# Graph network, four layers: the last chunk's adjacency in blocks of 32 rows, the reciprocals' transpose later, the first projection by quarters

## The chip, the cores and the metric

The kernel runs on one core of one Trainium2 chip. The metric is the device time of one execution in microseconds; smaller is better. Before and after are compared by the median of several executions.

## The reference

Four layers act on N = 2708 nodes with D = 512 features and a dense 2708 x 2708 adjacency matrix of zeros and ones, all in float32. The edits lie in layer 0, an attention layer with 8 heads of 64 dimensions:

```python
mask = adj, with ones on the diagonal
for h in range(8):
    q, k, v = x @ Wq[h], x @ Wk[h], x @ Wv[h]          # 2708 x 64 each
    s = where(mask > 0, q @ k.T / sqrt(64), -1e16)      # 2708 x 2708
    heads[h] = softmax(s, axis=-1) @ v                  # 2708 x 64
x = layernorm(x + sum(heads[h] @ Wo[h] for h in range(8)))
```

This is the computation in short form, with the mask as the kernel applies it. Layers 1 to 3 are a sum over neighbours with two linear maps, a second attention over the edges and a graph convolution scaled by node degree (the row sums of adj). They use the degrees that layer 0 collects on the way.

## The kernel before

**Tiling.** The nodes fall into NC = 22 chunks of 128 rows. The last chunk, LAST = 21, has only LR = 20 rows. The heads are taken as four pairs p; a pair's two heads are j = 0 and 1, in the lower and the upper 64 partitions. Over the columns of the score matrix there are three batches k: 1024, 1024 and 660 columns.

**The projections.** Before the attention, six blocks b of up to 512 nodes are projected to KT (psk), V (psv) and the queries (psq), which go to DRAM as qtd. `load_rows` brings a weight matrix or a block xb of the transposed features in one DMA of 1 MB. `project_in` multiplies, for one of four output groups p, the four feature quarters k into one PSUM tile; the pool ps_0 has four such tiles. `evac` copies to SBUF on DVE and ACT in turn.

**The attention loop.** It runs over items (c, p): 84 items for the 21 full chunks and one for the last chunk, in which four groups of 32 partitions hold the four pairs of heads of the 20 rows. Twelve of the 32 rows are filling: rows of chunk 20 that are computed and not used. An iteration works on several items at once: `scores` of the new item (PE products at line 310 and a fused add-and-maximum on DVE at L332), `weights` of the one before (exponentials on ACT, L354), `blocks` (transposes of 32 x 32 blocks on DVE, L361, into a tile d), `deal` (eight DMAs that reorder d into e, L371), `values` (products with V on PE, L417), and `turn` (PE transposes of the third batch, copied by ACT at L391 to L401). The results ot go to DRAM (otd), for the last chunk as otz (L481, L482).

**The next chunk's adjacency.** While the four items of chunk c run, `load_chunk(c + 1, p)` fetches one batch of adjacency columns per item (L167, for the last chunk L172) and, in the fourth item, the queries qt (L176, L178). `row_sums` adds up the batch on ACT into dgp (L185), from which the degrees come, `loops` puts ones on the diagonal (L197), and `mask` turns zeros into -1e16. For the last chunk, each of the four groups of 32 partitions gets the 20 real rows at its partitions 0 to 19, and 12 rows of chunk 20 behind them: two DMAs for each group and each batch.

**Sums and reciprocals.** The exponentials' sums are collected in smt. `heads_sums` adds them and forms reciprocals for the chunks 0 to 10 and later for 11 to 20 (L490, L495). `heads_rows` turns these by a PE transpose (prs, L503), copies them on ACT (rst, L505) and stores them to rs_d (L506). `last_sums` does so for the last chunk (L511 to L517: rz, prz, rstz, rz_d). The epilogue from L664 on loads otd, x and the reciprocals broadcast over 64 partitions (rb, L673), multiplies on POOL (L674), projects by wo on PE (L677) and normalises.

**Order.** Within the attention loop the order of PE, DVE and ACT is the order of the code. SP issues nearly all DMAs and POOL a few; on these two a scheduler orders the work by its own estimate of when it is ready. The degree computation (L595 to L600) is written after the loop; the scheduler places it on DVE and ACT within the last iterations. A queue works in order: a DMA whose issue waits holds what stands behind it. The main loop's lines:

```python
for i in range(len(items) + 3):
    ...
    if i in (HALF0 * NP + 2, len(items)):
        sums = heads_sums(i == len(items))
    if cur is not None:
        cur.turn()
    if i in (HALF0 * NP + 3, len(items)):
        heads_rows(*sums)
    if i == len(items) + 1:
        last_sums()
    old, late, cur = late, cur, new
```

Of the kernel before, what the change touches and what calls it, by code (L numbers as in the profile page):

```python
# [8 lines left out]
F32 = mybir.dt.float32  # L9
AF = mybir.ActivationFunctionType  # L10
# [5 lines left out]
P = 128  # L16
BLK = 512
# [5 lines left out]
def kernel(  # L23
# [22 lines left out]
    nc = tc.nc  # L46
    N, D = x.shape
    KD = 64
    NP = wq.shape[1] // P
    KC = D // P  # L50
# [4 lines left out]
    def rows(c):  # L55
        return c * P, min(P, N - c * P)
# [8 lines left out]
    const = ctx.enter_context(tc.tile_pool(name="const", bufs=1))  # L65
# [46 lines left out]
    def load_rows(t, src):  # L112
        nc.sync.dma_start(t, src.rearrange("(k p) f -> p k f", p=P))


    NW = 3
# [5 lines left out]
    nc.vector.memset(far, -1e16)  # L122
    dgp = const.tile([P, NC, NW], F32, tag="dgp", name="dgp")
    nc.vector.memset(dgp, 0.0)
    HALF0 = NC // 2
    smt = [const.tile([P, HALF0, 2 * NP, NW], F32, tag=f"smt{i}", name=f"smt{i}") for i in range(2)]
    for t in smt:
# [4 lines left out]
    rz_d = dram.tile([2, NP, 32], F32, tag="rz_d", name="rz_d")  # L132
    LAST = NC - 1
    LR = N - LAST * P
    otd = [dram.tile([P, NP, rows(c)[1]], F32, tag=f"otd{c}", name=f"otd{c}") for c in range(NC)]
    with ExitStack() as l0:
        kvp = l0.enter_context(tc.tile_pool(name="kv", bufs=1))
# [8 lines left out]
        qtd = [dram.tile([P, NP, rows(c)[1]], F32, tag=f"qtd{c}", name=f"qtd{c}") for c in range(NC)]  # L146
# [9 lines left out]
        def load_chunk(c, k):  # L156

            r0, q = rows(c)
            if k == 0:
                a = adjp.tile([P, N], F32, tag="adj", name=f"adj{c}")  # L160
                qt = io.tile([P, NP, P], F32, tag="qt", name=f"qt{c}")
                loaded[c] = (a, qt)
            a, qt = loaded[c]
            if k < NW:
                n0, w = batch(k)
                if c < LAST:
                    nc.sync.dma_start(a[:q, n0 : n0 + w], adj[r0 : r0 + q, n0 : n0 + w])  # L167
                    return

                for g in range(NP):  # L170
                    for d, r, n in ((0, r0, LR), (LR, N - 32, 32 - LR)):
                        nc.sync.dma_start(  # L172
                            a[32 * g + d : 32 * g + d + n, n0 : n0 + w], adj[r : r + n, n0 : n0 + w]
                        )
            else:
                nc.sync.dma_start(qt[:, :, :q], qtd[c])  # L176
                if c == LAST:
                    nc.sync.dma_start(qt[:, :, q:32], qtd[c - 1][:, :, P - (32 - q) :])  # L178

        def row_sums(c, k):  # L180

            r0, q = rows(c)
            a = loaded[c][0]
            n0, w = batch(k)
            nc.scalar.activation(  # L185
                a[:q, n0 : n0 + w], a[:q, n0 : n0 + w], AF.Copy, accum_out=dgp[:q, c, k : k + 1]
            )

        def loops(c, k):

            r0, q = rows(c)
            a = loaded[c][0]
            n0, w = batch(k)
            if n0 <= r0 < n0 + w:
                for g in range(0, P, 32) if c == LAST else (0,):
                    d = a[g : g + q, r0 : r0 + q]
                    nc.vector.tensor_tensor(d, d, ident[g : g + q, g : g + q], ALU.max)  # L197
# [7 lines left out]
        with tc.tile_pool(name="kvw", bufs=1) as kvw, tc.tile_pool(name="xTb", bufs=2) as xtp, tc.tile_pool(  # L205
            name="ps_0", bufs=4, space=PSUM
        ) as ps_0:
            wk_sb = kvw.tile([P, KC, D], F32, tag="wk", name="wk_sb")
            wv_sb = kvw.tile([P, KC, D], F32, tag="wv", name="wv_sb")
            wq_sb = kvw.tile([P, KC, D], F32, tag="wq", name="wq_sb")  # L210
            load_rows(wk_sb, wk)
            for b in range(NB):
                n0, w = cols(b)
                xb = xtp.tile([P, KC, BLK], F32, tag="xb", name=f"xb{b}")
                load_rows(xb[:, :, :w], xT[:, n0 : n0 + w])
                if b == 0:
                    load_rows(wv_sb, wv)
                    load_rows(wq_sb, wq)

                def project_in(w_sb, p, name):  # L220
                    ps = ps_0.tile([P, BLK], F32, tag="t", name=name)
                    for k in range(KC):
                        nc.tensor.matmul(  # L223
                            ps[:, :w],
                            w_sb[:, k, p * P : (p + 1) * P],
                            xb[:, k, :w],
                            start=(k == 0),
                            stop=(k == KC - 1),
                        )
                    return ps  # L230

                for p in range(NP):
                    ps = project_in(wk_sb, p, f"psk{b}_{p}")
                    evac(KT[:, p, n0 : n0 + w], ps[:, :w])


                xp = xtp.tile([P, KC, BLK], F32, tag="xp", name=f"xp{b}", bufs=1)
                for c in chunks_of(b):
                    o, q = rows(c)[0] - n0, rows(c)[1]
                    src = xb[:, :, o : o + q]  # L240
                    dst = xp[:, :, o : o + q]
                    if c < ND:
                        src = src.rearrange("p k (i x) -> p k x i", i=KD4)
                        dst = dst.rearrange("p k (x i) -> p k x i", i=KD4)
                    nc.gpsimd.tensor_copy(dst, src)
                for c in chunks_of(b):
                    r0, q = rows(c)
                    ps = ps_0.tile([P, BLK], F32, tag="t", name=f"psv{c}")
                    for k in range(KC):
                        nc.tensor.matmul(  # L250
                            ps[:q, :],
                            xp[:, k, r0 - n0 : r0 - n0 + q],
                            wv_sb[:, k, :],
                            start=(k == 0),
                            stop=(k == KC - 1),
                        )
                    evac(V[:q, c, :], ps[:q, :])
                qb = xtp.tile([P, NP, BLK], F32, tag="qb", name=f"qb{b}")
                for p in range(NP):
                    ps = project_in(wq_sb, p, f"psq{b}_{p}")  # L260
                    nc.scalar.mul(qb[:, p, :w], ps[:, :w], QSCALE)
                for c in chunks_of(b):
                    r0, q = rows(c)
                    nc.gpsimd.dma_start(qtd[c], qb[:, :, r0 - n0 : r0 - n0 + q])
                if b == NB - 3:
                    for k in range(NW + 1):
                        load_chunk(0, k)
                    for k in range(NW):
                        row_sums(0, k)
                        loops(0, k)  # L270
                        mask(0, k)

            ga_sb = kvw.tile([P, D], F32, tag="ga", name="ga_sb")
            pr = kvw.tile([P, D], F32, tag="pr", name="pr")
            nc.sync.dma_start(ga_sb, ga.partition_broadcast(P))
            for k in range(2 * KC):
                gw_sb = kvw.tile([P, D], F32, tag="gw", name=f"gw{k}", bufs=2)
                nc.sync.dma_start(gw_sb, gw[k * P : (k + 1) * P, :])
                nc.vector.tensor_tensor(pr, gw_sb, ga_sb, ALU.mult)
                nc.vector.tensor_reduce(u[:, k : k + 1], pr, AX.X, ALU.add)  # L280
# [159 lines left out]
        class Last(Pair):  # L440
# [18 lines left out]

            def weight(self, m, p, j):  # L460
                if m >= ND:
                    return self.pts[m, j][:, 32 * p : 32 * p + LR]
                f = max(f for f in self.E if f <= m)
                return self.E[f][:, p, j, m - f, :LR]

            def values(self, m0, m1):
                if self.done == 0:
# [52 lines left out]
        items = [(c, p) for c in range(LAST) for p in range(NP)] + [(LAST, 0)]  # L520
        old = late = cur = None
        with tc.manual_schedule(
            engines={mybir.EngineType.PE, mybir.EngineType.DVE, mybir.EngineType.Activation}
        ):
            for i in range(len(items) + 3):
# [4 lines left out]
                if i < len(items):  # L530
                    c, p = items[i]
# [35 lines left out]
                    sums = heads_sums(i == len(items))  # L567
                if cur is not None:
                    cur.turn()
                if i in (HALF0 * NP + 3, len(items)):  # L570
                    heads_rows(*sums)
                if i == len(items) + 1:
                    last_sums()
# [84 lines left out]
    with tc.tile_pool(name="wo", bufs=1, reuse_waits="tile") as wop:  # L658
        wo_sb = wop.tile([P, KC, D], F32, tag="wo", name="wo_sb")
        load_rows(wo_sb, wo)  # L660
        for c in range(NC):
            r0, q = rows(c)
# [4 lines left out]
            heads = rz_d if c == LAST else rs_d[c >= HALF0][c % HALF0]  # L667
            heads = heads.rearrange("j p q -> j (p q)")
            for j in range(2):
                dst = rb[j * KD : (j + 1) * KD]  # L670
                dst = dst[:, :, :32] if c == LAST else dst.rearrange("k p q -> k (p q)")
                src = rz_d[j] if c == LAST else heads[j]
                nc.sync.dma_start(dst, src.partition_broadcast(KD))  # L673
            nc.gpsimd.tensor_tensor(ot[:, :, :q], ot[:, :, :q], rb[:, :, :q], ALU.mult)  # L674
            po = ps_acc.tile([P, BLK], F32, tag="acc", name=f"po{c}")
# [122 lines left out]
    if True:  # L798
# [19 lines left out]
        for c in range(NC):  # L818
            q = rows(c)[1]
# [489 lines left out]
```

## Time and profile before

| what | us |
|---|---|
| median of 3 executions | 2607.38 |
| lowest and highest of the 3 | 2600.11 and 2610.36 |
| the profiled execution | 2611.59 |
| its span in the profile | 2609.8 |
| PE busy in the span | 2540.3 |
| DVE busy | 1874.5 |
| ACT busy | 1212.1 |
| POOL busy | 312.0 |

All times of the profile belong to that one execution and count from the start of its span. A row names the engine, the line of the kernel, the operation, its output and inputs, the shapes and how often (x). "[1.90 <-DVE rz L511]" means that the engine stood idle for 1.90 us before, and that the work named ended the idle time. The engines are PE (matrix products; PEld its weight loads), DVE, ACT, POOL and SP, which issues DMAs ("SPq" in the chain and in the rows of issues). "issue" as a releaser means that the profile shows nothing that was waited for. Ends of PE's records are modelled, so a busy PE is not always one at its peak.

### The profile page before, as it was taken

What the parts mean: (1) busy time and instruction counts of PE and PEld (TensorE: products, weight loads), DVE (VectorE), ACT (ScalarE), POOL (GpSimd) and SP (SyncE); (2) the same over time, 40 slices, a digit from 0 to 9 for tenths busy, and PEclk for the clock granted to TensorE, in tenths of its full rate; (3) what the DMA queues carried; (4) which work ended last, traced back from release to release, by engine and by line L of the source; (5) the groups of instructions that cost most, each with busy time, mean ns of one, the idle gap of its engine ahead of it and who ended that gap; (6) DMA issues with size and microseconds to landing.
All of it is one profiled execution on the core that took longest, in us unless ns stands there. A gap on an engine that the chain in (4) does not pass through costs nothing.

```text
span 2609.8 us, 42027 instructions
## 1 busy us (share of the span) xinstructions
PE 2540.3 (97%) x15263; PEld 1472.2 (56%) x15263; DVE 1874.5 (72%) x4576; ACT 1212.1 (46%) x2417; POOL 312.0 (12%) x322
## 2 busy tenths in 40 slices
PE   8999999999999999999899999899999999999997
PEld 3445666767676766676546444444444456444465
DVE  2004999999999999998484678978767775453544
ACT  1113778788787787887211001566555640000000
POOL 1110000000000000000220000234333330000000
PEclk9999999999999999999899999989999999999999
DMA  5012888888988888888772544354434213644633
GB/s 199 32 53 58 215 230 217 222 220 209 240 206 210 229 217 216 229 209 184 208 219 76 134 119 139 112 166 135 123 100 129 62 30 108 180 143 141 181 100 107
DMA packets 221445, 411.45 MB, mean 158 GB/s; under 512 B 28711, under 2 KB 48857, under 8 KB 221238
## 3 DMA queue, kind: packets, MB, share of 16 engines
q1 hardware_dynamic: 214998, 392.03, 56.3%
q0 software_dynamic: 6240, 16.73, 1.8%
q8 instruction: 121, 1.98, 0.3%
q14 instruction: 86, 0.70, 0.1%
HBM read 213.57 MB, written 16.72 MB: 88 GB/s over the span
## 4 chain that ended last, share of the span: by engine, by line
PE 77%; issue 9%; DVE 6%; DMA 4%; SPq 2%; ACT 1%; POOL 0%; POOLq 0%; DVEq 0%; ACTq 0%
PE pss L310 15%; PE av L417 14%; PE acc L731 13%; PE acc L837 7%; PE m L1141 6%; PE pf L743 3%; PE psv L250 3%; PE psk L223 3%; PE pst L390 3%; PE psq L223 3%; DMA e<-d 2%; PE po L677 2%; PE ph L823 1%; DVE d L361 1%; SPq L371 1%
## 5 line engine op out<-in xcount | busy, mean ns | idle before, releaser
L332 DVE CUSTOM_DVE_ANT_0 s<-pss,adj 128x512 f32<-128x512 f32 (+1 forms) x1020 | 574.2, 618 | 27.6 <-PE pss L310 26.5
L354 ACT ACTIVATE s<-s,nm 128x1024 f32<-128x1024 f32 (+1 forms) x510 | 527.7, 1037 | 22.9 <-DVE nm L347 22.0
L310 PE MATMUL pss<-KT,qt 64*128 64x512 f32 (+1 forms) x2016 | 463.8, 565 | 7.7 <-DVE mx L332 7.4
L361 DVE STREAM_TRANSPOSE d<-s 128x1024 f32<-128x1024 f32 x340 | 402.4, 1222 | 18.1 <-DMA e<-d 9.0
L731 PE MATMUL acc<-pt,x 128*128 128x512 f32 (+1 forms) x880 | 341.0, 547 | 12.6 <-ACT pt L784 9.7
L417 PEld LDWEIGHTS av<-e,V 128*64 128x64 f32 x5376 | 295.6, 137 | 62.6 <-issue 32.9
L417 PE MATMUL av<-e,V 128*64 128x128 f32 x5376 | 327.4, 275 | 0.0
L310 PEld LDWEIGHTS pss<-KT,qt 64*128 64x128 f32 x2016 | 194.2, 186 | 145.3 <-issue 69.3
L731 PEld LDWEIGHTS acc<-pt,x 128*128 128x128 f32 x880 | 161.1, 196 | 192.1 <-issue 166.0
L837 PE MATMUL acc<-at,h 128*128 128x512 f32 (+1 forms) x504 | 196.8, 543 | 0.0
L795 POOL TENSOR_TENSOR cs<-cs,pt 128x512 f32<-128x512 f32 (+2 forms) x110 | 157.3, 1430 | 202.8 <-ACT pt L784 199.5
L782 DVE TENSOR_TENSOR pt<-pt,at 128x512 f32<-128x512 f32 (+2 forms) x132 | 106.2, 812 | 80.7 <-ACT pt L781 80.5
L1171 ACT ACTIVATE z<-pz,rdeg 128x512 f32<-128x512 f32 (+1 forms) x22 | 15.1, 688 | 312.0 <-PE pz L743 312.0
L438 POOL DMA_DIRECT2D otd<-ot x84 | 45.2, 538 | 959.7 <-ACT ot L437 947.3
L93 ACT ACTIVATE ln_t<-lnve 128x1 f32<-128x1 f32 x88 | 17.7, 201 | 305.7 <-DVE lnve L107 305.7
L391 ACT COPY pt<-pst 128x512 f32<-128x512 f32 x170 | 91.5, 589 | 120.9 <-PE pst L390 120.5
L837 PEld LDWEIGHTS acc<-at,h 128*128 128x128 f32 x504 | 90.2, 190 | 101.4 <-issue 98.7
L417 PEld LDWEIGHTS av<-pt,V 128*64 128x64 f32 x1680 | 90.0, 136 | 64.6 <-ACT adj L185 46.2
L784 ACT ACTIVATE pt<-pt 128x512 f32<-128x512 f32 (+2 forms) x132 | 76.1, 578 | 106.8 <-DVE pt L783 106.6
L848 DVE SCALAR_TENSOR_TENSOR cs<-at,rdeg,cs 128x512 f32<-128x512 f32 (+2 forms) x126 | 86.2, 684 | 43.0 <-DMA at<-in_adjT_dram 41.7
L417 PE MATMUL av<-pt,V 128*64 128x128 f32 x1680 | 110.3, 278 | 1.4 <-ACT ot L437 1.4
L85 DVE COPY KT<-psk 128x512 f32<-128x512 f32 (+1 forms) x12 | 7.5, 629 | 139.5 <-PE psk L223 139.5
(297 smaller groups left out, 3560.4 us busy)
## 6 DMA issues: line engine op xcount, KB each, us to landing
e<-d SPq DMA_DIRECT2D x680, 256.0 KB
at<-in_adjT_dram SPq DMA_DIRECT2D x210, 256.0 KB
a<-in_adj_dram SPq DMA_DIRECT2D x38, 677.0 KB
adj<-in_adj_dram SPq DMA_DIRECT2D x42, 512.0 KB
at_a<-in_adjT_dram SPq DMA_DIRECT2D x40, 256.0 KB
at_c<-in_adjT_dram SPq DMA_DIRECT2D x40, 256.0 KB
at_f<-in_adjT_dram SPq DMA_DIRECT2D x40, 256.0 KB
adj<-in_adj_dram SPq DMA_DIRECT2D x21, 330.0 KB
```

The source lines that it names most:

```text
L223: nc.tensor.matmul(ps[:, :w], w_sb[:, k, p * P : (p + 1) * P], xb[:, k, :w], start=(k == 0), stop=(k == KC - 1),)
L310: nc.tensor.matmul(pss[j][:, :w], qt[h, self.p, :], KT[h, self.p, n0 : n0 + w], start=True, stop=True)
L332: nc.vector.tensor_tensor_reduce(out=s[:, j, h0 : h0 + hw], in0=pss[j][:, :hw], in1=a[:, n0 + h0 : n0 + h0 + hw], scale=1.0, scalar=LOW, o ...
L354: nc.scalar.activation(s, s, AF.Exp, bias=self.nm[j], accum_out=self.sums(j, k))
L361: nc.vector.transpose(self.D[k][:, :, j].rearrange("p i m x -> p m i x"), self.s[k][:, j, : n * P].rearrange("p (m i x) -> p m i x", i=KD4 ...
L391: nc.scalar.copy(sb, pt)
L417: nc.tensor.matmul(self.av[j * KD : (j + 1) * KD, out], V[:, m, h * KD : (h + 1) * KD], weights[j], start=(self.done == 0), stop=(self.don ...
L731: nc.tensor.matmul(acc[k][:, :w], last[0][g : g + mr, :] if m == NC - 1 else values[:mr, k * P : (k + 1) * P], moving[g : g + mr, :w], sta ...
L782: nc.vector.tensor_tensor(pt[:mr, :w], pt[:mr, :w], at[:mr, :w], ALU.subtract)
L795: nc.gpsimd.tensor_tensor(sums[:mr, :w], sums[:mr, :w], pt[:mr, :w], ALU.add)
L837: nc.tensor.matmul(acc[hc][:, :w], lastH[g : g + mr, :] if m == NC - 1 else H[m][:mr, hc * P : (hc + 1) * P], at[g : g + mr, :w], start=(m ...
L1141: nc.tensor.matmul(acc[k][:, : moving.shape[1]], combined[which, m][:, k * P : (k + 1) * P], moving, start=(m == 0), stop=(stop and m == N ...
```

## The change

It has three parts.

- The last chunk's adjacency is fetched as the last 32 rows of the matrix in one piece for each group of partitions: one DMA instead of two for each group and batch, 12 instead of 24. The real rows then stand at partitions 12 to 31 of each group, and the 12 filling rows (FILL) before them. Queries, weights and reciprocals of the last chunk are addressed accordingly. The row sums of the 32 rows go to a tile of their own, dgz, whose rows 12 to 31 a new DMA brings to partitions 0 to 19 of dgp.
- The second `heads_rows` comes one iteration later, behind the value products that are ready by then.
- In the first block, wk and xb are fetched in four quarters each, by features, and the 16 products run with the feature quarter in the outer loop, over four open PSUM tiles.

```diff
+    dgz = const.tile([P, NW], F32, tag="dgz", name="dgz")
...
+    FILL = 32 - LR
...
-                for g in range(NP):
-                    for d, r, n in ((0, r0, LR), (LR, N - 32, 32 - LR)):
-                        nc.sync.dma_start(
-                            a[32 * g + d : 32 * g + d + n, n0 : n0 + w], adj[r : r + n, n0 : n0 + w]
-                        )
+                for g in range(0, P, 32):
+                    nc.sync.dma_start(a[g : g + 32, n0 : n0 + w], adj[N - 32 :, n0 : n0 + w])
             else:
-                nc.sync.dma_start(qt[:, :, :q], qtd[c])
                 if c == LAST:
-                    nc.sync.dma_start(qt[:, :, q:32], qtd[c - 1][:, :, P - (32 - q) :])
+                    nc.sync.dma_start(qt[:, :, :FILL], qtd[c - 1][:, :, P - FILL :])
+                nc.sync.dma_start(qt[:, :, FILL:32] if c == LAST else qt, qtd[c])
...
-            nc.scalar.activation(
-                a[:q, n0 : n0 + w], a[:q, n0 : n0 + w], AF.Copy, accum_out=dgp[:q, c, k : k + 1]
-            )
+            dst = dgp[:, c, k : k + 1]
+            if c == LAST:
+                q, dst = 32, dgz[:, k : k + 1]
+            nc.scalar.activation(a[:q, n0 : n0 + w], a[:q, n0 : n0 + w], AF.Copy, accum_out=dst[:q])
+            if c == LAST and k == NW - 1:
+                nc.sync.dma_start(dgp[:LR, c, :], dgz[FILL:32, :])
...
+                if c == LAST:
+                    r0, q = N - 32, 32
                 for g in range(0, P, 32) if c == LAST else (0,):
                     d = a[g : g + q, r0 : r0 + q]
...
-            load_rows(wk_sb, wk)
             for b in range(NB):
                 n0, w = cols(b)
                 xb = xtp.tile([P, KC, BLK], F32, tag="xb", name=f"xb{b}")
-                load_rows(xb[:, :, :w], xT[:, n0 : n0 + w])
                 if b == 0:
+                    for k in range(KC):
+                        nc.sync.dma_start(wk_sb[:, k, :], wk[k * P : (k + 1) * P, :])
+                        nc.sync.dma_start(xb[:, k, :w], xT[k * P : (k + 1) * P, n0 : n0 + w])
                     load_rows(wv_sb, wv)
                     load_rows(wq_sb, wq)
+                else:
+                    load_rows(xb[:, :, :w], xT[:, n0 : n0 + w])
...
-                for p in range(NP):
-                    ps = project_in(wk_sb, p, f"psk{b}_{p}")
+                if b == 0:
+                    pk = [ps_0.tile([P, BLK], F32, tag="t", name=f"psk0_{p}") for p in range(NP)]
+                    for k in range(KC):
+                        for p in range(NP):
+                            nc.tensor.matmul(
+                                pk[p][:, :w],
+                                wk_sb[:, k, p * P : (p + 1) * P],
+                                xb[:, k, :w],
+                                start=(k == 0),
+                                stop=(k == KC - 1),
+                            )
+                else:
+                    pk = (project_in(wk_sb, p, f"psk{b}_{p}") for p in range(NP))
+                for p, ps in enumerate(pk):
                     evac(KT[:, p, n0 : n0 + w], ps[:, :w])
...
             def weight(self, m, p, j):
                 if m >= ND:
-                    return self.pts[m, j][:, 32 * p : 32 * p + LR]
+                    return self.pts[m, j][:, 32 * p + FILL : 32 * p + 32]
                 f = max(f for f in self.E if f <= m)
-                return self.E[f][:, p, j, m - f, :LR]
+                return self.E[f][:, p, j, m - f, FILL:]
...
-                if i in (HALF0 * NP + 3, len(items)):
+                if i in (HALF0 * NP + 3, len(items) + 1):
                     heads_rows(*sums)
...
-                dst = dst[:, :, :32] if c == LAST else dst.rearrange("k p q -> k (p q)")
-                src = rz_d[j] if c == LAST else heads[j]
+                dst = dst[:, :, :q] if c == LAST else dst.rearrange("k p q -> k (p q)")
+                src = rz_d[j, :, FILL:] if c == LAST else heads[j]
```

## The prediction

> **What bounds the kernel now.** I read the page, then the chain of waits, then the stretches around each edit: the start, the last chunk but one of layer 0 (1100 to 1250 us), and the end of layer 0 (1247 to 1275).
>
> ```profile
> PE 2540.3 (97%) x15263; PEld 1472.2 (56%) x15263; DVE 1874.5 (72%) x4576; ACT 1212.1 (46%) x2417; POOL 312.0 (12%) x322
> ...
> PE 77%; issue 9%; DVE 6%; DMA 4%; SPq 2%; ACT 1%; POOL 0%; POOLq 0%; DVEq 0%; ACTq 0%
> ```
>
> PE is busy nearly always, but its ends are modelled, so shares do not price a local edit; the stretch does. The start, from the chain:
>
> ```profile
> 1.27 7.82 DMA xb<-in_xT_dram
> ...
> 9.22 15.87 PE psk L223 x32
> 25.10 13.73 PE psv L250 x32
> ```
>
> PE stands still for 9.22 us until the whole 1 MB xb behind the whole 1 MB wk has landed; from there one projection follows the other (PE is busy 20.00 of 20.00 us from 20 to 40, 50.00 of 50.00 from 150 to 200, and DVE takes over at 233.8 without a gap). Next, stretches of one iteration of the attention loop (start:end, length, busy PE, PEld, DVE, ACT, POOL, then granted clock, DMA share, GB/s):
>
> ```profile
> 1162.54:1174.25 11.71, 11.71 (x125) 8.08 (x124) 11.26 (x32) 9.51 (x21) 0.54 (x1) 1.00 0.81 187
> 1174.25:1186.01 11.76, 11.76 (x126) 8.21 (x125) 11.62 (x31) 8.10 (x18) 0.54 (x1) 1.00 0.83 189
> 1186.01:1198.97 12.96, 11.78 (x126) 8.18 (x125) 10.94 (x29) 10.99 (x23) 0.54 (x1) 1.00 0.79 194
> 1198.97:1212.61 13.64, 12.56 (x124) 8.85 (x125) 11.46 (x31) 10.23 (x20) 0.54 (x1) 1.00 0.78 179
> 1212.61:1228.65 16.04, 13.67 (x124) 9.06 (x125) 12.80 (x41) 9.28 (x20) 0.54 (x1) 1.00 0.89 196
> ```
>
> Iterations cost 11.7 us until the last chunk's rows are fetched, then 12.96, 13.64, 16.04: 7.5 us over three times 11.71. What DVE waited for in 1186.5 to 1223 (total, times, longest):
>
> ```profile
> DVE d L361 <- issue: 2.5, 1, 2.5
> DVE d L361 <- ACT ot L437: 2.4, 2, 1.6
> ...
> DVE d L361 <- DMA e<-d: 1.4, 2, 0.8
> ```
>
> Those 6.3 us all stand ahead of the block transposes (L361), whose buffer d comes free when its e transfers have gone. The same view of 1100 to 1174 has 0.2. The reason, on SP (start, length):
>
> ```profile
> 1177.62 4.66 SPq L172 DMA_DIRECT2D adj<-in_adj_dram  x8
> 1182.39 8.81 SPq L371 DMA_DIRECT2D e<-d  x8
> 1191.24 5.09 SPq L172 DMA_DIRECT2D adj<-in_adj_dram  x8
> 1196.45 9.26 SPq L371 DMA_DIRECT2D e<-d  x8
> ```
>
> SP needs about 9 us for an iteration's eight e transfers; 4.7 to 5.1 for eight adjacency loads on top makes 13.5 to 14.5, over 11.7. In a usual chunk it issues three loads in all.
>
> The end of layer 0, PE and POOL, with the stretches behind it:
>
> ```profile
> 1251.18 0.28 PE L503 MATMUL prs<-ident,riTrue 128*80 128x128 f32 x1 [1.90 <-DVE rz L511]
> ```
> ```profile
> 1252.00:1254.00 2.00, 2.00 (x24) 2.00 (x22) 0.00 (x0) 0.00 (x0) 0.54 (x1) 0.53 0.97 230
> 1254.00:1255.50 1.50, 1.50 (x30) 1.50 (x28) 0.00 (x0) 0.27 (x1) 0.41 (x1) 0.50 0.88 245
> 1255.50:1258.00 2.50, 2.50 (x91) 2.50 (x89) 0.00 (x0) 0.00 (x0) 0.15 (x1) 1.00 0.91 199
> ```
> ```profile
> 1270.10 0.73 POOL L482 DMA_DIRECT2D otd<-otz  x1 [5.22 <-DMA rb<-rs_d]
> 1270.79 3.76 POOL L674 TENSOR_TENSOR otl<-otl,rb 128x512 f32<-128x512 f32 x3
> ```
>
> The transpose prs waits 1.90 us for DVE's sums and reciprocals; 32 ready value matmuls queue behind it. Then the clock is halved for some 3.4 us. POOL's first product of the epilogue stands behind otz, the last output, which ends the value matmuls.
>
> **The change, part by part.** *C, the first projection by quarters.* Two loads of 1 MB become eight of 256 KB, wk and xb alternating, and the first 16 matmuls run features outermost. PE can start when two quarters (0.52 MB) are in. By the stretches, DMA moved 158 GB/s in 2 to 3 us, then 377, 340, 373, 410: 0.58 MB are moved at 4.1 us. The full 2.1 MB were moved at about 8.1 and PE started 1.1 later. So PE starts at about 4.9 to 5.1, a gain of 4.2. Later quarters arrive every 1.4 us, while a quarter's four matmuls take at least 3.4 us (15.87 / 32 = 0.50 per record, two records a matmul): no starving. The cold clock, which lasts here about 3.8 us from the first matmul (weight loads 0.85 us apart until 12.8, then 0.43), may last up to 3 us longer, costing half of that at worst: take 0.2. Sum: 4.0, between 3.0 and 4.6; 0 if the quarters do not overlap. Costed at nothing because they lie beside PE: POOL's permuted copies of xb (4.06 us), wv behind it in the queue, and evacuation, where PSUM buffer 0 frees before the last of four is complete. From here to the attention loop nothing has slack, so the 4.0 should reach the end.
>
> Rule against it: 256 KB e transfers are issued at a median of 967 ns each, and the stretches show 340 to 410 GB/s with several loads in flight. The Trainium skill ("DMA: Bandwidth & Descriptors", anatomy of one DMA) prices a transfer at 2.0 us fixed plus bytes over 436 GB/s, fitted on another issue path, and asks to batch to a megabyte (rules for authors). By it 256 KB take 2.6 us; eight one after another 20.8, landing near 21.6 with psk ending near 25, gain 0. By the rows the fixed part overlaps. I follow the rows.
>
> *A, the adjacency in 32-row blocks.* 24 loads become 12, and SP's work falls by 12 x 0.61 us (14.56 / 24) = 7.3 us. But order counts: ahead of the end of iteration two's first e tile, SP had 16 loads (9.75 us); now it has the 12 loads plus both qt loads (6.9 + 2.6 = 9.5), moved up past e20_0_1 and e20_1. So the first two iterations gain little: by SP's count 0.25 us, by shorter bursts (five loads where eight stood together) more, of their 3.8 us of waits; I take 1.4. Behind them 4.8 us of loads and 2.6 us of qt are gone, which removes iteration three's 2.53. Removable is at most 6.3, DVE's waits; the degree chain's 1.4 busy and 0.54 waiting stay in iteration three. Less 0.5 for the store below: 1.4 + 2.5 - 0.5 = 3.4, between -0.9 (only the 1.4, and 2.3 of new stall) and 5.8 (6.3 less 0.5); when the stalls go, DVE itself (11.3 to 11.6 of 11.7) is next. The row sums and loops on 32 rows instead of 20 keep their element counts per partition, within 0.1 us in all. The four smaller rb elements: nothing.
>
> Added: a store dgp<-dgz, from ACT's last row sum, through SP, ahead of the degree reduction on DVE (L595, at 1223.86, T+11.2 with T the start of iteration three). Queued behind that: the fourth score of its group, the block transposes and their e transfers, then ACT's logarithm and PE's products. The sum ended at T+5.3. Without the 2.53 us stall L595 would stand at T+8.7. The trace has no such 240-byte transfer: nearest are small stores to DRAM, 2.9 to 4.2 us to landing; e transfers take 5.0 to 5.7. So it lands between T+8.3 and T+11 (5.3 + 5.7): 0 to 2.3 us of stall; I take 0.5, since a small store is the nearer row. It also adds one issue (0.3 to 1 us) to SP, covered by the loads that are gone.
>
> *B, the reciprocals' transpose moved.* prs now stands after the 64 first e products of the last chunk, ahead of prz; its copy on ACT and its store on POOL move past the last ot and otd. Removed: the idle 1.90 us; DVE's result, ready by 1251.18, is then there before PE comes to it; what PE can be late for next is the first e transfers of the last chunk. The halved clock follows the idle: the 32 av matmuls took 3.07 us against 1.97 in a usual iteration, and 3.4 us at half speed lose 1.7. prs's 0.28 stays. Sum 3.6, between 0 and 4.5. Upper end: rb's landing at 1266.22 holds POOL's product, which began at 1270.79. Lower: PE's 1.83 us stall without a named releaser at 1261.3, and e transfers issued until 1254.85. The later store delays rs_d[1] by about 10 us; it is first read from chunk 11 on, tens of us later: nothing.
>
> The rule for B: the trace halves the clock after 1.9 us of idleness. The skill ("TensorE: Matmul & The Clock Gate", Part 1) has the clock drop after an idle window of about 3.4 us. By it the drop was not this wait's doing, and B gives 1.9; by the rows, 3.6. I take the rows, since no other gap lies nearby.
>
> **Sum.** 4.0 + 3.4 + 3.6 = 11.0 us. The profiled execution is 2611.59 (span 2609.8 and 1.79 around it), so 2600.6 of that kind. It lies 4.2 above the median of the runs shown, 2607.38; the median after is 2596.4.
>
> **Rivals.** (1) All of it is recovered: A 5.8, B 4.5, C 4.6, 14.9 together: 2592.5. For: the stalls are absent in a usual chunk, which moves as many bytes. Against: SP stays crowded in the first two iterations. (2) One part yields nothing: either A, the backlog only moved forward, with dgp's wait in place of the old one (total 7.0 to 7.6: 2600); C, quarters in series (7.0: 2600.4); or B, PE held by e transfers or the 1.83 us stall (7.4: 2600). (3) Nothing reaches the end, another bound absorbing it: 2607. PE's unbroken chain speaks against it. (4) Slower: dgp<-dgz. DVE stops for it in the middle of iteration three, with PE and ACT behind. Price: its landing less T+8.7. From T+19.7 it eats all 11.0; from T+32.7 the kernel is 0.5% slower. This needs a wait of 14 us from sum to landing, or SP's queue blocked by its wait for ACT; rows of 3 to 6 us and its place after e20_1_1 speak against it.
>
> **How the numbers follow.** Half a per cent (13 us) is about what a measurement of this kernel tells from no change; the three runs span 10.2 us. Chances: forecast 0.49 (own range 8 to 14 us gained), rival 1 0.24, rival 2 0.16, rival 3 0.05, rival 4 0.06. Faster by over 0.5%, below 2594.3: most of rival 1 and a tail of the forecast, 0.31. Slower by over 0.5%: rival 4 and drift of rival 3, 0.06. Range 2588 to 2606: the low end is rival 1 less half the runs' span, the high end a gain of 1.4; left out are rivals 3 and 4 in the main and a little more.
>
> **What would show it.** C: PE's first matmul at about 5 us and psv beginning near 21; if near 25, wrong. A: iterations of about 12.3, 12.9 and 14 in place of 12.96, 13.64, 16.04, and no unnamed wait of 2.5 ahead of L361; a DVE wait of several us at the degree reduction on DMA dgp would prove rival 4. B: no gap at prs, clock 1.00 from 1249 on, the 32 av matmuls in 2.0 us, otz 3.6 us closer to the end of turn. Wrong in the whole if layers 1 to 3, whose orders stay as they were, change length.

## The result and the profile after

Six executions of the changed kernel took 2589.34 us in the median (2587.43 to 2591.52), six of the kernel before 2605.95 (2600.11 to 2610.36). The ratio is 0.9933 with a 95% interval of 0.9921 to 0.9945: 17 us less, between 14 and 21. The forecast was 2596.4 and 11.0 us less, the range 2588 to 2606. The profiled execution took 2589.45 us, with a span of 2587.7.

The start, from the chain of waits of the changed kernel:

```profile
1.21 2.81 DMA xb<-in_xT_dram
...
4.16 15.81 PE psk L243 x32
19.97 13.73 PE psv L269 x32
```

The first pair of quarters landed at 4.02 us. PE began at 4.16 in place of 9.22, and its 32 records took 15.81 us against 15.87: no quarter was waited for later and the cold clock cost no more. psv begins 5.13 us sooner, and the attention loop 5.15.

The three iterations beside the last chunk's loads (stretches, columns as before):

```profile
1176.29:1188.00 11.71, 11.71 (x126) 8.16 (x125) 10.86 (x29) 10.17 (x21) 0.54 (x1) 1.00 0.87 210
1188.00:1201.17 13.17, 12.19 (x125) 8.57 (x125) 11.41 (x31) 11.04 (x23) 0.54 (x1) 1.00 0.91 215
1201.17:1214.60 13.43, 12.20 (x124) 8.57 (x124) 12.74 (x41) 9.16 (x20) 0.54 (x1) 1.00 0.74 175
```

They take 11.71, 13.17 and 13.43 where they took 12.96, 13.64 and 16.04. SP, in the same time, start and length:

```profile
1167.58 3.40 SPq L173 DMA_DIRECT2D adj<-in_adj_dram  x5
1171.09 3.76 SPq L390 DMA_DIRECT2D e<-d  x4
1174.90 1.22 SPq L173 DMA_DIRECT2D adj<-in_adj_dram  x2
1176.22 3.78 SPq L390 DMA_DIRECT2D e<-d  x4
1180.06 4.04 SPq L173 DMA_DIRECT2D adj<-in_adj_dram  x5
```

The twelve loads take 8.66 us of SP in place of 14.56: 5.9 less, where the forecast had 7.3, since each of the larger loads takes 0.72 us and not 0.61. DVE, from its timeline of the changed kernel:

```profile
1198.34 2.37 DVE L380 STREAM_TRANSPOSE d<-s 128x1024 f32<-128x1024 f32 x2 [1.76 <-ACT s L373]
1209.82 0.22 DVE L614 TENSOR_REDUCE deg<-dgp 128x22 f32<-128x66 f32 x1
```

One wait of 1.76 us ahead of the block transposes is left in the second iteration. ACT's s, named as its releaser, was ready by 1195.9, and the chain of waits names nothing for 1.66 us of it; that it is for a d buffer, as before, is likely and not shown. The degree reduction behind the new store dgp<-dgz ran without any wait, 8.65 us after the start of its iteration: the store's landing cost nothing.

The end of layer 0, PE, ACT and POOL:

```profile
1235.17 1.97 PE L436 MATMUL av<-e,V 128*64 128x128 f32 x32
...
1245.14 0.41 PE L436 MATMUL avz<-e,V 128*64 128x20 f32 x7 [1.69 <-issue]
1245.49 0.31 PE L522 MATMUL prs<-ident,riTrue 128*80 128x128 f32 x1
1245.63 0.27 PE L533 MATMUL prz<-ident,rz 128*2 128x128 f32 x1
1245.83 5.72 PE L436 MATMUL avz<-e,V 128*64 128x20 f32 x118
1252.65 0.83 PE L436 MATMUL avz<-e,V 128*64 128x20 f32 x10 [1.09 <-issue]
```
```profile
1246.50:1248.00 1.50, 1.50 (x42) 1.50 (x38) 0.00 (x0) 0.00 (x0) 0.43 (x1) 0.64 1.10 350
1248.00:1249.00 1.00, 1.00 (x24) 1.00 (x24) 0.00 (x0) 0.00 (x0) 0.00 (x0) 0.50 0.94 248
```
```profile
1245.83 0.26 ACT L524 COPY rst<-prs 80x128 f32<-80x128 f32 x1 [8.38 <-PE prs L522]
1253.40 0.26 ACT L535 COPY rstz<-prz 2x128 f32<-2x128 f32 x1 [7.31 <-DMA rs_d<-rst]
1253.56 0.36 ACT L500 COPY otz<-avz 128x20 f32<-128x20 f32 x4
```
```profile
1253.94 0.52 POOL L536 DMA_DIRECT2D rz_d<-rstz  x1 [7.01 <-ACT otz L500]
1254.46 0.78 POOL L501 DMA_DIRECT2D otd<-otz  x1
1255.19 3.96 POOL L693 TENSOR_TENSOR otl<-otl,rb 128x512 f32<-128x512 f32 x3
```

The gap at prs is gone and the 32 records of the av products (two a product) take 1.97 us, at full clock. But 1.69 us without a named releaser remain in the first e products. The clock halves from 1246.9 on, as it did before from 1265.8, and now stays so past the end of the e products. And there is a wait that before did not have: rstz's copy stands for 7.31 us until the store rs_d<-rst has landed. In `heads_rows` and `last_sums` the two tiles have one tag with one buffer; rst is now filled just ahead of rstz. All four copies of otz and rz_d's store are late behind it.

Where the difference of the two profiles arises, by the starts of two DVE rows that each iteration or chunk has once (the maxima nm in the loop, bn_stats of the layer norm after it):

| stretch | before | after | less |
|---|---|---|---|
| start to the first nm | 240.38 | 235.23 | 5.15 |
| loop, iterations 0 to 80 | 946.14 | 941.57 | 4.57 |
| iterations 80 to 84, the last chunk's loads | 54.91 | 50.58 | 4.33 |
| end of layer 0, to the first layer norm | 37.14 | 35.69 | 1.45 |
| the rest, to the last layer norm | 1319.97 | 1313.32 | 6.65 |

The three edited stretches give 10.9, nearly the forecast sum. The loop and the rest, whose instructions are the same in the same order, give 11.2 more; that layers 1 to 3 changed length is the sign by which the prediction would be wrong in the whole. This before was profiled in an execution 5.6 us above its median. Where the rest of the 11.2 comes from was the question of the experiments.

### The profile page after: what moved, and what is told of

Read it like the earlier page. It is cut to its first block, busy times and chain, and to the rows that moved or that the text cites. A ratio compares the mean times of both kernels' runs of the same rounds, so it can differ in the third digit from the quotient of the medians.

```text
span 2587.7 us, 42022 instructions
## 1 busy us (share of the span) xinstructions
PE 2532.2 (98%) x15263; PEld 1468.0 (57%) x15263; DVE 1874.8 (72%) x4576; ACT 1211.7 (47%) x2417; POOL 314.0 (12%) x322
## 4 chain that ended last, share of the span: by engine, by line
PE 79%; issue 9%; DVE 7%; DMA 2%; ACT 1%; SPq 1%; POOL 0%; POOLq 0%; DVEq 0%; ACTq 0%
PE pss L329 15%; PE av L436 15%; PE acc L750 13%; PE acc L856 7%; PE m L1160 6%; PE pf L762 3%; PE psv L269 3%; PE pst L409 3%; PE psq L230 3%; PE psk L230 2%; PE ph L842 1%; PE acc_0a L750 1%; DVE d L380 1%; DMA e<-d 1%; DVE s L351 1%
## 5 line engine op out<-in xcount | busy, mean ns | idle before, releaser
L380 DVE STREAM_TRANSPOSE d<-s 128x1024 f32<-128x1024 f32 x340 | 402.4, 1222 | 9.4 <-DMA e<-d 6.5
```

Source lines behind the costliest of these rows:

```text
L380: nc.vector.transpose(self.D[k][:, :, j].rearrange("p i m x -> p m i x"), self.s[k][:, j, : n * P].rearrange("p (m i x) -> p m i x", i=KD4 ...
```

## The experiments

Ratios are against the kernel before, run beside each kernel on the same chip; us are worked out as the ratio's distance from 1 times the median of before there (2606.45, 2604.55 and 2605.16 us for the three sets).

| kernel | ratio (95%) | us less | loop 0 to 80 | iterations 80 to 84 | end of layer 0 |
|---|---|---|---|---|---|
| c_only | 0.9981 (0.9967 to 0.9994) | 5.0 | 948.36 | 53.10 | 39.36 |
| a_only | 0.9957 (0.9940 to 0.9973) | 11.2 | 941.40 | 51.23 | 42.17 |
| b_only | 0.9995 (0.9984 to 1.0006) | 1.3 | 946.51 | 55.79 | 35.33 |
| after_rstz | 0.9918 (0.9905 to 0.9932) | 21.4 | 942.08 | 50.25 | 35.41 |
| after_again | 0.9931 (0.9917 to 0.9944) | 18.0 | 942.19 | 51.05 | 35.25 |
| no_c | 0.9957 (0.9943 to 0.9971) | 11.2 | 941.98 | 49.79 | 36.15 |
| no_a | 0.9973 (0.9961 to 0.9985) | 7.0 | 947.79 | 53.99 | 34.45 |
| a24 | 0.9984 (0.9972 to 0.9996) | 4.2 | 941.25 | 57.14 | 40.34 |
| pad_only | 0.9966 (0.9953 to 0.9979) | 8.9 | 943.29 | 51.69 | 40.41 |
| after_pad32 | 0.9957 (0.9945 to 0.9969) | 11.2 | 948.36 | 53.44 | 35.44 |
| after_pad224 | 0.9953 (0.9938 to 0.9969) | 12.2 | 947.30 | 51.67 | 33.27 |
| best | 0.9943 (0.9931 to 0.9955) | 14.8 | 943.98 | 53.00 | 34.17 |

**The parts alone.** Each is the kernel before with one part of the diff shown above: c_only with the eight quarter loads and the products by quarters, a_only with the 32-row blocks, dgz and FILL, b_only with this line:

```diff
-                if i in (HALF0 * NP + 3, len(items)):
+                if i in (HALF0 * NP + 3, len(items) + 1):
```

> The kernel before with part C alone (quarters of wk and xb, feature quarter outermost). Theory, the gains are local: PE's first product moves from 9.22 to about 4.2 us and every later instruction by the same 5.1 to 5.2, so 5 us under before, with the last chunk's iterations still near 13.0, 13.6 and 16. Rival, the start also sets how transfers meet in the loop and in layer 2: the iterations 0 to 79 and the stretch 1650 to 1950 us shorten as they did in the profile of after (4.6 and 6.9 us there), 10 us or more in all.

> The kernel before with part A alone (32-row blocks, dgz). Its order up to the last chunk's loads is that of before. Theory: iterations 81 to 83 gain 4.3 us, 4 us under before in all, and the iterations 0 to 79 agree with before to within chance. If they are shorter than in the profile of before by several us although no instruction there differs, then that profile's extra time is chance and not an effect of the change. Rival: removing loads gives 8 us or more, through later layers.

> The kernel before with part B alone (the transpose prs one iteration later). Theory: 1.5 us at the first po, as between the two profiles: the 1.9 us gap and the half clock behind it go (3.7 us at the first e products), and some of it is lost again before otz, where the rstz copy waits for the rs_d store to land because both copies share one buffer. 1 to 2 us under before. Rival: the loss in after came from its own transfers, and alone B gives 3.6.

C gave its 5.0 and nothing above it: loop 948.36, iterations 80 to 84 53.10, within what kernels without A show (53.1 to 55.8). A gave 11.2, which the rival had, and its stretch is only 3.7 us shorter than in before. The theory's second sentence fell too: the loop is 4.7 us shorter with A, and again in every later kernel with A's own layout, so it was not chance. B alone gave 1.3, not to be told from nothing. Its stretch was 35.33 against 37.14 in before, 1.8.

The layers after the epilogue do vary by chance. Two stretches of 20 us of layer 2 in before, then the same work in b_only:

```profile
1722.77:1742.77 20.00, 17.16 (x34) 7.11 (x33) 14.29 (x31) 9.47 (x14) 8.86 (x4) 0.83 0.48 156
1742.77:1762.77 20.00, 17.64 (x52) 8.39 (x51) 14.38 (x21) 12.31 (x20) 8.54 (x4) 0.83 0.33 101
```
```profile
1719.84:1739.84 20.00, 17.20 (x44) 7.66 (x43) 13.65 (x29) 8.94 (x13) 8.86 (x4) 1.00 0.45 152
1739.84:1759.84 20.00, 17.64 (x62) 8.81 (x62) 18.00 (x25) 14.83 (x23) 10.23 (x5) 1.00 0.40 115
```

The clock granted in them was 0.83 in one execution and 1.00 in the other, with nothing changed there. From layer norm 42 to 54 the fourteen profiles range from 320.3 to 328.6 us, in no order that follows an edit. Of the 6.65 us that the rest gave between the first two profiles, 6.1 lie there. Over all fourteen profiles the rest takes 1313.2 us in the mean of the eight kernels whose loop is short and 1313.7 in the mean of the other six: it is chance.

**Two parts together, and the changed kernel again.** no_c and no_a are the changed kernel with the hunk of C or of A (and for A all that serves it) taken back.

> The changed kernel itself once more, for its spread. The stretches that the change touches gave 5.15 (start), 4.3 (last chunk) and 1.5 us (end of layer 0), 11.0 together; the measured median gave 16.6. If the other 5.6 are chance of those few executions (the half clock behind the waits of layer 2, the loop's contention, both of which differ by up to 9 us between profiles of kernels with the same order there), these runs spread over 10 us, with a median nearer to 11 under before. If they come with the change, the median is again 15 to 18 under before.

> The changed kernel without part C (parts A and B). If parts only act where they are made: 5 to 6 us under before by the stretches of the profile. If what lies above the stretches comes with A, as A alone measured 11.2 under before with 3.7 in its stretch: 12 to 13.

> The changed kernel without part A (parts B and C). Local: 5.1 + 1.5 = 6.6 us under before, and C alone (5.0) and B alone (1.3) say the same. If the extra comes with A: the same 6 to 7. If it comes from any change of the start times: 10 or more.

The changed kernel repeats: 18.0 less, with a spread of 5 us. A with B gives 11.2, B with C 7.0: the extra comes with A, wherever A is.

**Does the number of loads make it?**

```diff
-                    nc.sync.dma_start(a[g : g + 32, n0 : n0 + w], adj[N - 32 :, n0 : n0 + w])
+                    for h0, h1 in ((n0, n0 + w // 2), (n0 + w // 2, n0 + w)):
+                        nc.sync.dma_start(a[g : g + 32, h0:h1], adj[N - 32 :, h0:h1])
```

> Part A alone with each load halved by columns: 24 loads again, of 32 rows and 512 or 330 columns, the same bytes. Theory, the stall is SP's time to issue: 24 issues bring it back, iterations 81 to 83 take about 13 to 13.6 and 16 us again in all (42.6 in before, 39.9 in A alone), and A's gain in this stretch goes. Rival, the pieces of 20 and 12 rows were slow themselves: the gain of 3 to 4 us stays with 24 loads of 32 rows.

With 24 loads the stall is back in the first two iterations, 15.48 and 16.58 us by nm where a_only has 12.65 and 13.49. From SP's timeline of a24:

```profile
1172.48 5.21 SPq L174 DMA_DIRECT2D adj<-in_adj_dram  x9
1177.80 3.88 SPq L376 DMA_DIRECT2D e<-d  x4
1181.72 2.58 SPq L174 DMA_DIRECT2D adj<-in_adj_dram  x4
1184.42 4.87 SPq L376 DMA_DIRECT2D e<-d  x4
1189.34 6.38 SPq L174 DMA_DIRECT2D adj<-in_adj_dram  x11
```

All 24 are issued from 1172.48 to 1195.72, with only eight e transfers between them, which is worse than the order of before (57.14 for 54.91). So SP's time to issue does delay d, as the prediction had it. The third iteration stays short (13.71 us, as in a_only): all loads are past by then. Yet the loop keeps its 941.25: what shortens the loop in kernels with A is not the loads.

**The addresses.** What a_only and a24 share in the loop with the changed kernel, and c_only, b_only and no_a do not, is the tile dgz. It takes 32 bytes per partition ahead of nearly all other tiles. By the addresses in the compiled programs, d starts at 181984 and 190176, e at 198368, 206560 and 214752 in before: 224 past a multiple of 256. With dgz all of them move by 32, to multiples of 256. (So do the other tiles of the loop, s and KT among them, from 224 to 0; V, qt and adj move from other starts.) The DMA queue's row for 300 to 1100 us (packets, MB, share of 16 engines' time), before and after:

```profile
q1 hardware_dynamic: 87547, 169.61, 84.2%
```
```profile
q1 hardware_dynamic: 88104, 170.64, 81.7%
```

The DMA engines move more bytes in less of their time: 0.496 points of share per MB before, 0.479 after, 3.6% less. The test is the kernel before with only an unused tile in dgz's place, and the changed kernel with one more tile of 32 bytes, or of 224 (56 floats), at the same place:

```diff
     nc.vector.memset(dgp, 0.0)
+    pad = const.tile([P, NW], F32, tag="pad", name="pad")
+    nc.vector.memset(pad, 0.0)
```

> The kernel before with one more tile of three floats per partition in the place where part A puts dgz, set to zero and not used. It moves every tile behind it by 32 bytes: d and e, between which most of the loop's DMA traffic runs, start at 0 past a multiple of 256 bytes, as in the changed kernel, and not at 224. Theory, the tiles' addresses: the loop's DMA share falls from 84 to 82% as in every kernel with part A, iterations 0 to 80 take 941 to 942 us and not 946 to 948, 5 to 7 us under before with no other change. Rival, the gain above the stretches is made by part A's loads: no difference.

> The changed kernel with one more tile of 224 bytes: d and e start at 224 past a multiple of 256, as in before. Theory, the addresses: the loop takes 946 to 948 us again, DMA share 84%, and the changed kernel keeps only what its stretches show, 10 to 12 us under before in place of 17. Rival: no difference to the changed kernel.

> The changed kernel with one more tile of 32 bytes behind dgp: d and e start at 32 past a multiple of 256. If alignment to 64 bytes or the number of 256-byte pieces that a row of 2 KB touches (9 for 8) counts, the loop goes back to 946 to 948 us and the kernel loses 5 to 7 us to the changed one. [...]

pad_only, after_pad224 and after_pad32, the same row:

```profile
q1 hardware_dynamic: 87892, 170.25, 81.9%
```
```profile
q1 hardware_dynamic: 87429, 169.40, 84.4%
```
```profile
q1 hardware_dynamic: 87502, 169.53, 82.9%
```

An unused tile makes the kernel before 8.9 us faster (5 to 12). With 224 bytes of nothing the changed kernel gives 12.2 where it had given 17 and 18.0; these were measured in different sets, and the intervals overlap a little, so in time the way back is likely and not clear of noise. The loop, one profile of each kernel, separates without overlap: 941.3 to 944.0 us in the eight kernels with d and e at multiples of 256, 946.1 to 948.4 in the six without; means 942.2 and 947.4. The start at 32 lies between by busy time (0.489 points per MB); by the loop (948.36) and by the median (11.2) it is as slow as the start at 224. So of the three starts that were tried, 0, 32 and 224, the saving came with 0.

Could it be that engines, and not DMA, read or write faster at the new addresses? The two rows of the block transposes from 300 to 1100 us, before and pad_only (busy, mean ns of one, then DVE's idle time before them), say no:

```profile
L361 DVE STREAM_TRANSPOSE d<-s 128x1024 f32<-128x1024 f32 x270 | 319.5, 1222 | 7.8 <-DMA e<-d 4.0 <-ACT ot L437 1.9 <-issue 1.9
```
```profile
L363 DVE STREAM_TRANSPOSE d<-s 128x1024 f32<-128x1024 f32 x272 | 321.9, 1222 | 4.7 <-DMA e<-d 3.3 <-ACT ot L439 1.1 <-issue 0.2
```

One transpose takes 1222 ns in both, as one exponential takes 1139, one score record 615 and one record on e 274. What shrinks is DVE's wait ahead of the transposes, 7.8 to 4.7 us; it is 4.0 in the changed kernel, 9.0 in after_pad224 and 9.4 in after_pad32. Which tile's address matters was not taken apart; that it is d and e rests on their share of the transfers.

**A buffer for rstz, and a last version.**

```diff
-            rst = small.tile([P, P], F32, tag="rst", name="rstz", bufs=1)
+            rst = small.tile([P, P], F32, tag="rstz", name="rstz", bufs=1)
```

> The changed kernel with a buffer of its own for rstz (tag rstz in place of the shared rst), so that this copy no longer waits for the rs_d store. Theory: rstz is copied at once behind prz, 7 us sooner, the three first otz copies and rz_d's store leave the end, and the first POOL product starts 0.5 to 1 us sooner; 0.5 to 1 us under the changed kernel. Rival: the end waits for PE's last products alone, whose half clock and 1.1 us stall stay: no difference.

The wait is gone (ACT and POOL of after_rstz):

```profile
1247.08 0.25 ACT L535 COPY rstz<-prz 2x128 f32<-2x128 f32 x1
```
```profile
1247.42 0.54 POOL L525 DMA_DIRECT2D rs_d<-rst  x1 [8.20 <-ACT rstz L535]
1247.95 0.52 POOL L536 DMA_DIRECT2D rz_d<-rstz  x1
1254.51 0.76 POOL L501 DMA_DIRECT2D otd<-otz  x1 [6.04 <-ACT otz L500]
1255.24 1.33 POOL L693 TENSOR_TENSOR otl<-otl,rb 128x512 f32<-128x512 f32 x1
```

From the end of PE's last e product to POOL's product it is 1.25 us (PE ended at 1253.99) against 1.71 in the changed kernel (1253.48) and 2.53 in b_only (1267.18 to 1269.71). The median, 2586.16 us, is the lowest of all, but its interval overlaps those of the changed kernel; half a us to one is less than these runs tell apart. The last version also puts adj and qt at multiples of 256:

```diff
+        pad = kvp.tile([P, 48], F32, tag="pad", name="pad")
+        nc.gpsimd.memset(pad, 0.0)
...
-                a = adjp.tile([P, N], F32, tag="adj", name=f"adj{c}")
+                a = adjp.tile([P, N + 44], F32, tag="adj", name=f"adj{c}")
```

> The changed kernel with a buffer of its own for rstz, and with qt and adj also at multiples of 256 bytes (adj tiles 44 floats wider, a tile of 192 bytes ahead of qt); d and e stay at multiples. adj and qt are some 15% of the loop's bytes. Theory: 0.5 to 1.5 us under the changed kernel by rstz and up to 1 more by the addresses, about 18 to 19 us under before. Rival: no difference to the changed kernel, since these loads do not bound the loop.

It is no faster than the changed kernel (14.8 less): the rival held. Nor can its median be told from after_pad224's, which was run beside it (12.2). The version to keep is the changed kernel, with rstz's own buffer as a repair whose gain is seen in the trace alone.

## Why the prediction was right or wrong

**C: right in mechanism, 1.1 us too small.** Forecast 4.0, measured 5.15 in the profile and 5.0 in time. The mis-sized term is the way from bytes moved to PE's start. The prediction had 0.58 MB moved at 4.1 us and added 0.8 to 1.0, the lag of the 1 MB loads. In the changed kernel 0.58 MB were moved at 3.8 us (266 GB/s from 2 to 3 us, where before had 158), and PE began 0.4 later. The 0.2 for a longer cold clock was not needed. The Trainium skill's price for one transfer alone ("DMA: Bandwidth & Descriptors", anatomy of one DMA), 2.6 us for 256 KB, is near the 2.81 of the first xb quarter; what did not come is the sum of eight in series, which gave no gain. The rows were right to follow.

**A: the sum of 3.4 came near, and only in part for its reasons.** Between the first two profiles iterations 80 to 84 gave 4.33, with 1.25, 0.46 and 2.61 for the three in question. But pad_only gets 3.2 of it, at 51.69 us, with all 24 loads of before. Kernels with A and d and e at multiples of 256 stand at 49.8 to 51.2 (a24 aside, and best, whose adj lies elsewhere, at 53.0). At the old alignment, no A: 53.1 to 55.8, with A: 51.7 and 53.4. So of the term "1.4 + 2.5" about 1 to 2 us are the loads', and 1 to 3 the addresses'; a_only's time over pad_only's, 2.3 us, agrees, with an uncertainty of about 5. That fewer issues free SP, and that SP's order keeps the first two iterations from gaining much, a24 and the profile bear out. The 2.5 of the third iteration came as forecast: it takes 13.7 us in seven of the nine kernels with A (14.7 and 14.8 in best and after_pad32) and 15.2 to 16.6 in the five without, with 15.2 in pad_only. The term of 0.5 for dgp<-dgz was nothing, and rival 4 with it.

**B: the removed part was sized right, what came next was not named.** The 1.90 us gap and the half clock behind it went, 3.8 us at the first e products (1257.58 less 1239.74, less the 14.05 that the earlier parts had brought). At the first layer norm 1.45 were left. Of the difference, 1.7 us are lost within the e products: from their first to their last they take 13.73 us, 12.01 before, with the half clock over more of them and a second stall of 1.09. Another 0.5 is lost from their end to POOL's first product (1.71 us for 1.20), and that is the step that failed: "the later store delays rs_d[1]... nothing". The store was weighed for rs_d's readers, and not for the buffer that rst and rstz share. It is worth about 0.5 to 1.3 us, by after_rstz. In time B alone gave 1.3 (up to 4.2). The profiled executions show more, 33.3 to 36.1 us in nine kernels with B and 37.1 to 42.2 in five without, but four of these five were profiled in executions 5.6 to 10.3 us above their medians; how much of B's gain unprofiled executions have stays open between 0 and 4 us.

**The clock.** The five kernels without B wait 1.86 to 2.67 us for prs; in each the granted clock falls to half for 3.4 us, from 0.2 us before the end of that wait to 0.9 behind it. In the nine with B both are absent. So here a gap of 1.9 us was enough, as the prediction had it from the rows, where the skill's idle window of about 3.4 us ("TensorE: Matmul & The Clock Gate", Part 1) would have let it pass. The second halving, among the last chunk's e products, is another matter. It comes in all fourteen profiles, 1.8 to 8.2 us behind their first, and it does not follow the stall that stands there. In after_pad224 no gap is longer than 0.26 us, and the clock falls all the same (first fence). In a_only it falls at the start of the stall, not behind it (second fence). Columns as in the prediction's stretches:

```profile
1248.10:1251.50 3.40, 3.14 (x103) 3.01 (x99) 0.00 (x0) 0.00 (x0) 0.00 (x0) 1.00 0.92 243
1251.50:1254.90 3.40, 3.40 (x57) 2.97 (x58) 0.00 (x0) 0.26 (x1) 0.54 (x1) 0.50 0.96 320
```
```profile
1250.60:1254.00 3.40, 3.33 (x115) 3.23 (x111) 0.00 (x0) 0.00 (x0) 0.00 (x0) 1.00 0.91 269
1254.00:1258.10 4.10, 0.00 (x0) 0.00 (x0) 0.00 (x0) 0.00 (x0) 0.00 (x0) 0.50 1.05 299
```

What halves it stays open. What is common to all is the run of products of 20 columns ahead of it.

**The sum: right in part by luck.** 11.0 were forecast, 17 measured. The time lies within the range 2588 to 2606, but near its low end, and not within the 8 to 14 us to which the prediction gave its 0.49. The sum took the loop and all that was not edited as unchanged in length. The tile dgz was costed as a DMA and a wait, not as 32 bytes that move every tile behind it: 5 us in the loop's 80 iterations, and in time 8.9 by pad_only and about 5 to 6, within noise, by after_pad224. Without it (after_pad224) the change gives 12.2, between 8 and 16, the forecast's size. Rival 1's 14.9 was passed, but not by its mechanism: the stalls in the last chunk were not all recovered.

A page offers a reason: the skill ("DMA: Bandwidth & Descriptors", how a descriptor splits into AXI transactions) has a transfer cut at multiples of 256 bytes, so that a row of 2 KB which starts elsewhere needs nine pieces for eight. By its beats an estimate is 71 for 64 at a start of 224 and 65 at 32, or 11% and 1.6% more. Measured were 3.6% of the DMA engines' time at 224 and about 2% at 32, and equal time of the loop. The direction agrees, the sizes do not. That the pieces are the mechanism is argued from the page; that the loop's time follows the addresses is shown.

## What to carry to other kernels

A new tile, however small, moves the addresses of all tiles allocated behind it: before a gain or a loss is put down to an edit's instructions, run the old kernel with an unused tile of the same size in the same place. Where the DMA engines of a loop are as busy as here (82 to 84%), try the alignment of the tiles that carry most bytes; here multiples of 256 were better than starts 32 and 224 behind one. When a copy or store is moved later, ask which buffer it holds and who fills that next, not only who reads its result.

## What the runs showed of the hardware

- A shift of 32 bytes in the start of d and e, and of the tiles around them, changed the DMA engines' busy time per byte by 3.1% (pad_only) to 3.6% (the changed kernel) and the loop by 5 us of 947, with each engine's instructions as long as before.
- With PE gaps of 1.86 to 2.67 us ahead of prs the granted clock fell to half for 3.4 us, in five kernels of five; without these gaps it did not, in nine of nine. In the run of 20-column products behind, it fell in all fourteen, also where no gap was longer than 0.26 us.
- Stretches of layer 2 with the same work in the same order ran at a granted clock of 0.83 in one execution and 1.00 in another, and that part of the kernel took 320.3 to 328.6 us.
- The run of 20-column products stalls without a releaser that the profile shows: 0.7 to 4.3 us in eleven of fourteen profiles, each time behind 119 to 122 records of the first e products, and 0.26 us there in after_pad224. The cause is open.
- A load of 256 KB with others in flight landed 2.8 us after its issue, and eight in a row kept PE fed.
